# One state's product moved to GpSimd, one product with dt moved by six units, and feed-forward blocks issued together at both ends

## The chip, the core and the metric

The kernel runs on one core of one Trainium2 chip. The engines are called by the names of the profile: PE is TensorE (matmul), DVE is VectorE, ACT is ScalarE, POOL is GpSimd, SP is SyncE, which here only issues DMAs. The metric is the device time of one execution in microseconds (us), lower is better; "time" without more is the median of several executions.

## What is computed

Two layers of a metaformer on x of shape (2, 96, 128, 128). Each layer normalizes over the channels, mixes, adds the result to x, normalizes again, and adds a quantized feed-forward network. Layer 0 mixes with four state-space scans (rows and columns, forwards and backwards), layer 1 with a 3x3 convolution:

```
x = x + mamba4(_ln_c(x))          # four directions, joined by fuse_w
t = t + _L0_ffn_ref(_ln_t(t))     # 96 -> 384 -> 96, fp8 inputs, fp16 accumulator rounding
x = x + conv3x3(_ln_c(x))         # the same 3x3 kernel form as a full 96x96 convolution
t = t + _L1_ffn_ref(_ln_t(t))
```

One scan direction has 192 channels with 16 states each and runs over 16384 positions:

```
h = dA * h + dt_t[:, :, None] * B_t[:, None, :] * u_t[:, :, None]    # dA = exp(dt_t * A)
y = jnp.einsum('bds,bs->bd', h, C_t)
```

then y + D*u, times silu(z), times an output matrix.

## The kernel before

**Order.** For each of the two images, `tile_metaformer` runs `normalize`, then `mamba`, then `ffn_and_conv`. In all three the order of the instructions of each engine is the order in which the program issues them (`in_order`). An engine works strictly through its own list, so a waiting instruction holds back all that stand behind it.

**The scan part, `mamba`.** Two directions run at the same time as a pair (PAIRS): 384 channels in three groups g of 128 partitions. The positions are cut into tiles of T = 512. One **step** is one tile of one pair; there are 64 steps for an image, 128 in all. A step has 24 **units**: 3 groups times 8 pairs of states (g, s), so unit 0 is (0, 0), unit 8 is (1, 0), unit 10 is (1, 4), unit 16 is (2, 0). For unit k the program issues, over several turns of the loop at L486:

- POOL, once for two units (`feed` calls `b_part`, L349): B times dt*u for four states, [128, 4, 512] (L350), and the entry state into the first column (L354, with L353 where s = 0). It is issued two units ahead.
- ACT (`decay`, L360): two exponentials da = exp(dt*A) of [128, 512] into PSUM, issued two units ahead; three such buffers go round (`ps_w`), so the exponentials of unit k+3 write over da of unit k.
- DVE (`scan`, L364): one recurrence for each of the two states.
- `behind` (L453), one unit later: the product with C (L459, DVE, both states in one instruction of 1024 columns), an ACT copy of the last column of h into `hst` (L460), and PE matmuls with the identity that add both states into y (`sums`, L368).

In the six units of BY_POOL (s = 0 and 8 of each group: units 0, 4, 8, 12, 16, 20) the scan writes into the B tile in SBUF instead of PSUM, and POOL makes the product with C (L371, issued at turn k+1); the sums follow at turn k+3. Beside this run the steps of the next tile's preparation, each with a turn: the input matmuls (L218), their copies (L250, L258), two silu passes, each with two table loads (`silu`, L269 to L271; in the steady state they stand at turns 7 and 11), softplus, and `dt_u` (L307): dt times u for one group on POOL, at turns 19, 27 and 29 of the preparation, that is units 19, 3 and 5 of the steps. SP fetches the B and C rows (`row_tile`, L346) into 5 and 4 buffers.

**The part after it, `ffn_and_conv`.** 32 tiles of 512 positions go through four stages: feed-forward of layer 0 (`ffn(0, r)`), layer norm and padding (`to_pad(r)`), convolution (`conv(r)`), feed-forward of layer 1 (`ffn(1, r)`). Each stage is a generator that yields between its short pieces of work. `together` takes a list of (turn at which to begin, generator) and issues one piece of each per turn, in the order of the list; a call of `together` ends when all of its generators have. A feed-forward block has 11 turns: mean removal (xm, L124), square, variance (v, L130), logarithm and exponential, xq (L138), first matrix (L579) in two turns, ReLU, second matrix (L598), copy (L601), and the addition to x on POOL (L604). `to_pad` has the first five of these, the last with three POOL operations (L640 to L643). `conv` issues 12 matmuls (each is two PE instructions), one a turn, and four DVE additions (L625 to L629). The stages are joined by 36 calls, the first and the last four of which hold less than all stages:

```
stages = ((0, 0, partial(ffn, 0)), (4, 4, partial(ffn, 1)), (1, 8, to_pad), (3, 1, conv))
for r in range(NT + 4):
    together(*((at, f(r - lag)) for lag, at, f in stages if 0 <= r - lag < NT))
```

Of the kernel before, what the change touches and what calls it, by code (L numbers as in the profile page):

```python
# [15 lines left out]
ALU = mybir.AluOpType  # L16
# [7 lines left out]
T = 512  # L24
NT = L // T
# [9 lines left out]
ROW_BUFS = (5, 4)  # L35
AHEAD = 2
BY_POOL = tuple((g, s) for g in range(3) for s in (0, 8))
BCO = 32
SEG = 8
NBC = 4 * S  # L40
# [3 lines left out]
def tile_metaformer(ctx: ExitStack, tc: tile.TileContext, a: dict, out: bass.AP):  # L44
    nc = tc.nc
# [94 lines left out]
    def together(*streams):  # L140

        turn = 0
        streams, done = list(streams), object()
        while streams:
            left = []
            for at, g in streams:
                if turn < at or next(g, done) is not done:
                    left.append((at, g))
            streams = left
            turn += 1  # L150
# [40 lines left out]
    def mamba(acc, xnr, xnc, pools, heads):  # L191

        with ExitStack() as st:
            pool = lambda n, bufs, **kw: st.enter_context(tc.tile_pool(name=n, bufs=bufs, **kw))
# [6 lines left out]
            hst = one.tile([128, NG, S], F32, name="hst")  # L201
# [19 lines left out]
            def prologue(pi, i, d):  # L221
# [4 lines left out]
                lo = L - (i + 1) * T if rev else i * T  # L226
# [91 lines left out]
                at = [(-3, 1, load), (3, 0, partial(mix, "xc")), (11, 0, partial(silu, "xc"))]  # L318
# [9 lines left out]
                    at += [(k, 1, partial(softplus, x0, x1))]  # L328
                for g, k in enumerate((14, 24, 25) if first else (14, 15, 16)):
                    at += [(k, 0, partial(dt_in, g)), (k + 1, 0, partial(dt_out, g))]  # L330
                for g, k in enumerate((19, 27, 29)):
                    at += [(k, 0, partial(dt_u, g))]
                    if i > 0:
                        at += [((20, 24, 29)[g], 1, partial(entry, g))]

                outs = (conv_out, gate_out, rows_out, dt_out)
                at = [(k, where, getattr(f, "func", f) not in outs, f) for k, where, f in at]
# [23 lines left out]
                return da  # L361

            def scan(j, da, b, h):
                nc.vector.tensor_tensor_scan(h[:, j, :], da[:, j, :], b[:, j, :], 0.0, ALU.mult, ALU.add)  # L364

            def sums(s, y, c):
                for j in range(2):
                    nc.tensor.matmul(y, ident, c[:, j, :], start=False, stop=s + j == S - 1)  # L368

            def by_pool(h, c):  # L370
                nc.gpsimd.tensor_tensor(c, h, c, ALU.mult)  # L371

            def gated(pi, d, g, y):
                t = d["sz"][:, g, :]
# [26 lines left out]
            def later(k, where, rank, f, *args):  # L401
                todo.setdefault((k, where), []).append((rank, partial(f, *args)))
# [40 lines left out]

            ys = {}

            def gate_before(k):
                pn, pu = divmod(k - 1, nu)
                gated(steps[pn][0], state[pn], units[pu][0], ys.pop(k - 1))
# [4 lines left out]
            def behind(k):  # L453

                n, u = divmod(k, nu)
                (pi, i), d, (g, s) = steps[n], state[n], units[u]
                h, c = hs.pop(k), cs.pop(k)
                if (g, s) not in BY_POOL:
                    nc.vector.tensor_tensor(c, h, c, ALU.mult)  # L459
                nc.scalar.copy(hst[:, g, s : s + 2], h[:, :, T - 1])  # L460
                if s == 0:
                    if k > 0:
                        gate_before(k)
                    y = ps_y.tile([128, T], F32, name="y")
                    nc.tensor.matmul(y, dmat[:, pi, g, :], d["xc"][:, g, :], start=True, stop=False)  # L465
                else:
                    y = ys.pop(k - 1)
                ys[k] = y
                if (g, s) in BY_POOL:
                    later(k + 1, 1, True, by_pool, h, c)  # L470
                    later(k + 3, 1, True, sums, s, y, c)
                else:
                    sums(s, y, c)
                if k == total - 1:
                    gated(pi, d, g, y)
                if s == S - 2 and g > 0:
                    later(k + 4, 0, True, project, pi, i, d, g)
                    later(k + 5, 1, False, collect, pi, d, g)
# [7 lines left out]
            for k in range(total + 6):  # L486
                n, u = divmod(k, nu)
                if u == nu - 3:

                    prepare(n + 2)  # L490
                if k % 2 == 0:
                    fetch(k + 2 * B_AHEAD, 0, bs)
                    feed(k + AHEAD)
                issue(k, 0)
                if k < total:
                    (g, s) = units[u]
                    da, b = das.pop(k), bs.pop(k)
                    hs[k] = b if (g, s) in BY_POOL else da
                    scan(0, da, b, hs[k])
                if 0 < k <= total and not begins(k - 1):  # L500
                    behind(k - 1)
                feed_decay(k + AHEAD)
                if k < total:
                    scan(1, da, b, hs[k])
                if begins(k - 1):
                    behind(k - 1)
                if k % 2 == 0:
                    fetch(k + 2 * C_AHEAD, 1, cs)
                issue(k, 1)

    def ffn_and_conv(b, acc):

        with ExitStack() as st:
# [53 lines left out]
            def ffn(n, r):  # L567

                w1, w2, b1, b2 = layers[n]
                x = acc[:, r * T : (r + 1) * T]  # L570
                xq = wp.tile([C, T], F8, name="xq")
                yield from layernorm(x, eps_t[0:C, 0:1], xq, wp, psp, saturate=False)
                yield
                ph, h16 = [None] * 3, [None] * 3
                hq = wp.tile([128, 3, T], F8, name="hq")

                def up(m):
                    ph[m] = psp.tile([128, T], F32, name="ph", bufs=2)
                    nc.tensor.matmul(ph[m], w1[:, m * 128 : (m + 1) * 128], xq, start=True, stop=True)  # L579

                def half(m):
                    h16[m] = wp.tile([128, T], F16, name="h16", bufs=6)
                    nc.scalar.copy(h16[m], ph[m])

                def relu(m):
                    nc.vector.tensor_scalar(h16[m], h16[m], b1[:, m : m + 1], 0.0, ALU.add, ALU.max)
                    nc.vector.tensor_copy(hq[:, m, :], h16[m], saturate=False)

                up(0), up(1)
                yield  # L590
                half(0), half(1), up(2)
                yield
                relu(0), relu(1), half(2)
                yield
                relu(2)
                po = psp.tile([C, T], F32, name="po", tag="v")
                for m in range(3):
                    nc.tensor.matmul(po, w2[:, m, :], hq[:, m, :], start=m == 0, stop=m == 2)  # L598
                yield
                y16 = wp.tile([C, T], F16, name="y16")  # L600
                nc.scalar.copy(y16, po)  # L601
                yield
                nc.vector.tensor_scalar(y16, y16, b2[:, 0:1], None, ALU.add)  # L603
                nc.gpsimd.tensor_tensor(x, x, y16, ALU.add)  # L604
                if n == 1:
                    nc.sync.dma_start(out[b, :, r * T : (r + 1) * T], x)
                    if b + 1 < NB and r > 4 and r % 4 == 1:
                        read(b + 1, acc, r // 4 - 1)

            def conv(r):  # L610

                seg, lo = segs[r // SEG], r % SEG * R
                x = acc[:, r * T : (r + 1) * T].rearrange("c (n k) -> c k n", k=2)

                def products(name, k0):
                    pc = psp.tile([C, 2, R * half_w], F32, name=name, bufs=1)
                    for k in range(2):
                        for ky in range(3):
                            rows = seg[:, k0 + k, lo + ky : lo + ky + R, :]
                            nc.tensor.matmul(pc[:, k, :], uw[:, k0 + k, ky, :], rows, start=ky == 0, stop=ky == 2)  # L620
                            yield
                    return pc

                outer = yield from products("pc0", 0)
                nc.vector.tensor_tensor(x, x, outer, ALU.add)  # L625
                inner = yield from products("pc1", 2)
                nc.vector.tensor_tensor(x, x, inner[:, 0:1, :].broadcast_to((C, 2, R * half_w)), ALU.add)
                for k, op in enumerate((ALU.add, ALU.subtract)):
                    nc.vector.tensor_tensor(x[:, k, :], x[:, k, :], inner[:, 1, :], op)  # L629
# [17 lines left out]
                    nc.gpsimd.tensor_copy(segs[q - 1][:, :, seg_r + 1, :], segs[q][:, :, 1, :])  # L647

            stages = ((0, 0, partial(ffn, 0)), (4, 4, partial(ffn, 1)), (1, 8, to_pad), (3, 1, conv))
            for r in range(NT + 4):  # L650
                together(*((at, f(r - lag)) for lag, at, f in stages if 0 <= r - lag < NT))

    for b in range(NB):
        xnr = dpool.tile([C, L], F32, name="xnr")
# [78 lines left out]
```

## Time and profile before

| What | us |
|---|---|
| three timed runs | 11155.13, 11156.58, 11157.98; median 11156.58 |
| the profiled execution, its own time | 11158.01 |
| its span, first to last instruction | 11156.2 |
| scan part of each image, 97.8 to 5067.0 and 5660.0 to 10638.0 | 4969.2 and 4978.0 |
| `ffn_and_conv` of each image, 5067.0 to 5582.9 and 10638.0 to 11156.2 | 515.9 and 518.2 |
| one step of the scan part in the steady state | 77.36 |
| busy in the span: PE, DVE, ACT, POOL | 92%, 94%, 71%, 88% |

The page gives busy time per engine over the span; groups of instructions by line with their mean duration; and a chain of work that ended last, followed back from the end, which names at each point the engine that the end really depended on. The trace behind it answers the same for a stretch of time: a list of one engine's instructions with start, duration and the idle time ahead of them, or the pieces of the chain within the stretch. An instruction's duration is longer than the distance to the next one where the engine overlaps them: the 512 column scans last 1.22 us and start every 1.12 us.

### The profile page before, as it was taken

How to read it: one execution, taken by the hardware profiler on the slowest of the kernel's cores; microseconds unless marked ns; L12 is line 12 of the kernel's file. 1: busy time of each engine (PE TensorE's matmuls, PEld its weight loads, DVE VectorE, ACT ScalarE, POOL GpSimd, SP SyncE). 2: the span in 40 equal slices, each digit the busy share in tenths (PEclk: the TensorE clock that was granted, in tenths of full speed). 3: DMA queues.
4: the chain of work that ended last, by engine and by line, in shares of the span. 5: the costliest groups of instructions: out<-in, count | busy, mean ns of one | idle time of the engine just before them, and what ended most of it. 6: DMA issues, size and time to landing. Idle time of an engine off the chain costs nothing.

```text
span 11156.2 us, 94135 instructions
## 1 busy us (share of the span) xinstructions
PE 10260.0 (92%) x24592; PEld 3999.1 (36%) x24592; DVE 10498.1 (94%) x10337; ACT 7927.3 (71%) x13564; POOL 9803.2 (88%) x4908
## 2 busy tenths in 40 slices
PE   8999999999999999998989999999999999999988
PEld 3333333333333333334433333333333333333344
DVE  7999999999999999996579999999999999999955
ACT  6777777777777777775677777777777777777756
POOL 6999999999999999993269999999999999999932
PEclk9999999999999999999999999999999999999999
DMA  8888888888888888881178888888888888888800
GB/s 307 340 336 338 344 338 342 335 339 344 336 344 336 339 343 336 341 337 45 29 283 340 340 339 342 337 337 343 339 340 339 336 344 339 340 339 336 341 31 15
DMA packets 540497, 3416.18 MB, mean 306 GB/s; under 512 B 67469, under 2 KB 68589, under 8 KB 143577
## 3 DMA queue, kind: packets, MB, share of 16 engines
q1 hardware_dynamic: 539160, 3408.84, 78.0%
q8 instruction: 199, 3.26, 0.1%
q14 instruction: 338, 2.76, 0.1%
q10 hardware_dynamic: 800, 1.31, 0.0%
HBM read 3288.26 MB, written 54.53 MB: 300 GB/s over the span
## 4 chain that ended last, share of the span: by engine, by line
DVE 55%; issue 18%; ACT 18%; PE 8%; DMA 0%; POOL 0%; DVEq 0%; SPq 0%; POOLq 0%; ACTq 0%
DVE da L364 33%; DVE row L364 10%; DVE row L459 9%; ACT da L360 5%; ACT L270 3%; ACT L271 3%; PE pc L620 2%; PE v L130 2%; PE xm L124 2%; ACT xc L270 2%; ACT sz L270 2%; PE ph L579 1%; DVE sz L375 1%; ACT xc L250 1%; ACT mix L258 1%
## 5 line engine op out<-in xcount | busy, mean ns | idle before, releaser
L350 POOL TENSOR_TENSOR row<-dtu,row 128x2048 f32<-128x2048 f32 x1536 | 6950.6, 4526 | 7.5 <-DMA row<-bcd 7.0
L368 PE MATMUL y<-row,ident 128*128 128x512 f32 x12288 | 5684.5, 602 | 360.8 <-DVE row L459 350.8
L364 DVE TENSOR_TENSOR_SCAN da<-da,row 128x512 f32<-128x512 f32 x4608 | 5497.9, 1216 | 82.4 <-ACT da L360 35.0
L360 ACT ACTIVATE da<-dt,amat 128x512 f32<-128x512 f32 x6144 | 4247.9, 693 | 176.6 <-DVE row L364 6.3
L368 PEld LDWEIGHTS y<-row,ident 128*128 128x128 f32 x12288 | 2251.2, 190 | 3668.3 <-issue 2249.7
L459 DVE TENSOR_TENSOR row<-da,row 128x1024 f32<-128x1024 f32 x2304 | 2772.2, 1203 | 0.0
L371 POOL TENSOR_TENSOR row<-row,row 128x1024 f32<-128x1024 f32 x768 | 1806.5, 2352 | 271.0 <-issue 149.0
L460 ACT COPY hst<-da 128x2 f32<-128x2 f32 x2304 | 373.5, 162 | 2272.4 <-DVE row L459 2269.5
L364 DVE TENSOR_TENSOR_SCAN row<-da,row 128x512 f32<-128x512 f32 x1536 | 1849.6, 1204 | 34.4 <-DMA row<-bcd 32.1
L218 PE MATMUL misc<-xa,inx 96*64 96x512 f32 (+1 forms) x2048 | 935.1, 599 | 13.2 <-ACT dt L300 6.4
L218 PE MATMUL misc<-xb,inx 96*64 96x512 f32 (+1 forms) x2048 | 935.0, 599 | 1.6 <-ACT xc L250 1.6
L309 POOL TENSOR_TENSOR dtu<-dt,xc 128x512 f32<-128x512 f32 x384 | 488.2, 1271 | 188.1 <-ACT dt L304 102.3
L604 POOL TENSOR_TENSOR acc<-acc,y 96x512 f32<-96x512 f32 x128 | 147.1, 1149 | 547.0 <-DVE y L603 547.0
L383 PE MATMUL misc<-acc,ident 96*96 96x512 f32 x512 | 388.2, 843 | 222.1 <-ACT hst L460 199.3
L218 PEld LDWEIGHTS misc<-xa,inx 96*64 96x64 f32 (+1 forms) x2048 | 323.9, 163 | 581.1 <-issue 474.1
L465 PE MATMUL y<-xc,dmat 128*128 128x512 f32 x768 | 420.1, 628 | 110.5 <-DVE sz L375 110.5
L295 PE MATMUL misc<-rows,dtw 12*128 12x512 f32 x768 | 434.0, 645 | 64.4 <-ACT dt L300 35.5
L385 PE MATMUL misc<-sz,gmat 128*96 128x512 f32 x1024 | 483.6, 594 | 0.0
L620 PE MATMUL pc<-seg,uw 96*96 96x256 f32 x1536 | 424.5, 381 | 1.9 <-POOL seg L640 1.9
L218 PEld LDWEIGHTS misc<-xb,inx 96*64 96x64 f32 (+1 forms) x2048 | 323.4, 163 | 251.1 <-issue 186.3
L354 POOL TENSOR_TENSOR row<-row,enter 128x4 f32<-128x4 f32 x1488 | 298.2, 200 | 116.5
L277 PE MATMUL misc<-xc,bcw 128*96 128x512 f32 x768 | 355.8, 600 | 7.2 <-ACT xc L270 7.2
(92 smaller groups left out, 7423.0 us busy)
## 6 DMA issues: line engine op xcount, KB each, us to landing
row<-bcd SPq DMA_DIRECT2D x3072, 1024.0 KB, 7.4
xc<-mix SPq DMA_DIRECT2D x252, 128.0 KB, 4.8
sz<-mix SPq DMA_DIRECT2D x252, 128.0 KB, 4.8
xa<-xnr SPq DMA_DIRECT2D x124, 193.1 KB, 5.1
xb<-xnc SPq DMA_DIRECT2D x124, 193.1 KB, 5.5
bcd<-rows SPq DMA_DIRECT2D x126, 128.0 KB, 4.2
acc<-in_x_dram SPq DMA_DIRECT2D x16, 768.0 KB, 5.7
xnr<-xn SPq DMA_DIRECT2D x16, 768.0 KB, 4.9
```

The costliest lines, as they stand in the source:

```text
L218: nc.tensor.matmul(ps[rows, :], w(PAIRS[pi][d], k, lo, hi), src[d][:, k : k + T], **se)
L270: nc.scalar.activation(d[name], d[name], AF.Silu)
L295: nc.tensor.matmul(d["ps"], w, d["rows"][0 : 2 * RK, :], start=True, stop=True)
L309: nc.gpsimd.tensor_tensor(dtu, d["dt"][:, g, :], d["xc"][:, g, :], ALU.mult)
L350: nc.gpsimd.tensor_tensor(b, d["dtu"][g][:, None, :].broadcast_to((128, 4, T)), b, ALU.mult)
L360: nc.scalar.activation(da[:, j, :], d["dt"][:, g, :], AF.Exp, scale=amat[:, pi, g, s + j : s + j + 1])
L364: nc.vector.tensor_tensor_scan(h[:, j, :], da[:, j, :], b[:, j, :], 0.0, ALU.mult, ALU.add)
L368: nc.tensor.matmul(y, ident, c[:, j, :], start=False, stop=s + j == S - 1)
L371: nc.gpsimd.tensor_tensor(c, h, c, ALU.mult)
L385: nc.tensor.matmul(d["po"], gmat[:, pi, 2 * g - 2 + k, :], d["yg"][g - 1 + k], start=False, stop=k == 1)
L459: nc.vector.tensor_tensor(c, h, c, ALU.mult)
L620: nc.tensor.matmul(pc[:, k, :], uw[:, k0 + k, ky, :], rows, start=ky == 0, stop=ky == 2)
```

## The change

1. `HALF_POOL` names one unit, (1, 4), which is unit 10. Its first state is scanned into the B tile and multiplied by C on POOL (512 columns, issued at turn k+1 = 11); its second state stays as it was, with a DVE product of 512 columns instead of 1024. The one ACT copy into `hst` becomes two copies of one column each. The first state's sum on PE moves to turn k+3 = 13.
2. `dt_u` of group 2 moves from turn 29 to turn 35 of the preparation: from unit 5 to unit 11 of the step, ahead of the new POOL product.
3. In `ffn_and_conv` the first three calls of `together` become one and the last four become one. In the last one `conv` issues three matmuls per turn instead of one.

```
+HALF_POOL = ((1, 4),)
...
-                for g, k in enumerate((19, 27, 29)):
+                for g, k in enumerate((19, 27, 35)):
                     at += [(k, 0, partial(dt_u, g))]
...
-            def sums(s, y, c):
-                for j in range(2):
+            def sums(s, y, c, states=(0, 1)):
+                for j in states:
                     nc.tensor.matmul(y, ident, c[:, j, :], start=False, stop=s + j == S - 1)
 
-            def by_pool(h, c):
-                nc.gpsimd.tensor_tensor(c, h, c, ALU.mult)
+            def product(engine, h, c, states):
+                if len(states) == 2:
+                    engine.tensor_tensor(c, h, c, ALU.mult)
+                for j in states if len(states) == 1 else ():
+                    engine.tensor_tensor(c[:, j, :], h[:, j, :], c[:, j, :], ALU.mult)
...
+            def by_pool(g, s):
+                return (0, 1) if (g, s) in BY_POOL else (0,) if (g, s) in HALF_POOL else ()
...
-                h, c = hs.pop(k), cs.pop(k)
-                if (g, s) not in BY_POOL:
-                    nc.vector.tensor_tensor(c, h, c, ALU.mult)
-                nc.scalar.copy(hst[:, g, s : s + 2], h[:, :, T - 1])
+                (da, b), c = hs.pop(k), cs.pop(k)
+                pool = by_pool(g, s)
+                rest = tuple(j for j in (0, 1) if j not in pool)
+                if rest:
+                    product(nc.vector, da, c, rest)
+                for h, states in ((b, pool), (da, rest)):
+                    if states:
+                        lo, hi = states[0], states[-1] + 1
+                        nc.scalar.copy(hst[:, g, s + lo : s + hi], h[:, lo:hi, T - 1])
...
-                if (g, s) in BY_POOL:
-                    later(k + 1, 1, True, by_pool, h, c)
-                    later(k + 3, 1, True, sums, s, y, c)
-                else:
-                    sums(s, y, c)
+                if pool:
+                    later(k + 1, 1, True, product, nc.gpsimd, b, c, pool)
+                    later(k + 3, 1, True, sums, s, y, c, pool)
+                if rest:
+                    sums(s, y, c, rest)
...
-            def conv(r):
+            def conv(r, burst=1):
...
-                            yield
+                            if (3 * k + ky + 1) % burst == 0:
+                                yield
...
-            for r in range(NT + 4):
-                together(*((at, f(r - lag)) for lag, at, f in stages if 0 <= r - lag < NT))
+            together(*((2 * r, ffn(0, r)) for r in range(3)), (11, to_pad(0)), (13, to_pad(1)))
+            for r in range(3, NT):
+                together(*((at, f(r - lag)) for lag, at, f in stages if 0 <= r - lag))
+            together(
+                (0, to_pad(NT - 1)), *((at, ffn(1, NT - 4 + k)) for k, at in enumerate((0, 5, 11, 15))),
+                *((at, conv(NT - 3 + k, 3)) for k, at in enumerate((0, 6, 10))),
+            )
```

More of the change, by code (lines that the diff above doesn't have):

```diff
@@ L363, in scan @@
             def scan(j, da, b, h):
-                nc.vector.tensor_tensor_scan(h[:, j, :], da[:, j, :], b[:, j, :], 0.0, ALU.mult, ALU.add)
-            def sums(s, y, c):
-                for j in range(2):
+                nc.vector.tensor_tensor_scan(h[j], da[:, j, :], b[:, j, :], 0.0, ALU.mult, ALU.add)
+            def sums(s, y, c, states=(0, 1)):
+                for j in states:
                     nc.tensor.matmul(y, ident, c[:, j, :], start=False, stop=s + j == S - 1)
-            def by_pool(h, c):
-                nc.gpsimd.tensor_tensor(c, h, c, ALU.mult)
+            def product(engine, h, c, states):
[3 more added lines that the diff above has]
+                    engine.tensor_tensor(c[:, j, :], h[:, j, :], c[:, j, :], ALU.mult)
             def gated(pi, d, g, y):
@@ L497, in mamba @@
                     da, b = das.pop(k), bs.pop(k)
-                    hs[k] = b if (g, s) in BY_POOL else da
-                    scan(0, da, b, hs[k])
+                    hs[k] = da, b
+                    h = [(b if j in by_pool(g, s) else da)[:, j, :] for j in range(2)]
+                    scan(0, da, b, h)
                 if 0 < k <= total and not begins(k - 1):
@@ L503, in mamba @@
                 if k < total:
-                    scan(1, da, b, hs[k])
+                    scan(1, da, b, h)
                 if begins(k - 1):
```

## The prediction

> **What bounds the kernel now.** I read the shares of the chain first. DVE is 94% busy, but the chain gives it 55% and ACT 18%, though ACT is only 71% busy. So somewhere the end waits for ACT.
>
> ```profile
> DVE 55%; issue 18%; ACT 18%; PE 8%; DMA 0%; POOL 0%; DVEq 0%; SPq 0%; POOLq 0%; ACTq 0%
> ```
>
> POOL has 0%: in the steady state nothing waits for its 88%. Then I took the chain's pieces in one step of the scan part, and looked for where ACT enters. In this step unit 10's first scan starts at 2075.00, unit 13's at 2085.37.
>
> ```profile
> 2075.00 0.06 DVE da L364
> 2075.06 1.08 issue
> 2076.14 1.22 DVE row L459
> 2077.36 0.02 issue
> 2077.38 0.17 ACT hst L460
> 2077.55 0.02 issue
> 2077.57 0.70 ACT da L360
> 2078.28 0.02 issue
> 2078.30 0.69 ACT da L360
> 2079.00 0.61 ACT xc L250
> 2079.60 0.02 issue
> 2079.62 1.28 ACT L270
> 2080.90 0.01 issue
> 2080.91 1.49 ACT xc L270
> 2082.41 0.02 issue
> 2082.42 1.28 ACT L271
> 2083.70 0.01 issue
> 2083.72 0.17 ACT hst L460
> ```
>
> The reader should see what is missing. The chain leaves DVE with the product of unit 9 (2076.14) and stays on ACT: copy, exponentials of unit 12, xc, silu between two table loads, unit 10's hst copy, and (2083.91 to 85.34) the exponentials of unit 13. It comes back to DVE at 2085.37. DVE's product of unit 10, at 2079.51, is not on it. DVE's own list shows the wait at its return (last bracket):
>
> ```profile
> 2079.51 1.21 DVE L459 TENSOR_TENSOR row<-da,row 128x1024 f32<-128x1024 f32 x1
> ...
> 2085.37 1.23 DVE L364 TENSOR_TENSOR_SCAN da<-da,row 128x512 f32<-128x512 f32 x1 [0.17 <-ACT da L360]
> ```
>
> The other ACT stretch runs from unit 6's product (2065.97) to 2075.00, through the other silu; DVE waits 0.24 there. Some steps name POOL's L371 as releaser of that wait; but at 4086.26 the same scan starts before that POOL product ends (4084.08 + 2.35 = 4086.43), so it is ACT. Both waits recur every 77.36 us in the five stretches I read, so one step is DVE from 2085.37 to the next unit 6, then ACT, a little DVE, and ACT.
>
> For the feed-forward ends I read the engines' lists and the granted clock by stretch.
>
> ```profile
> 5069.50:5113.90 44.40, 32.68 (x47) 9.52 (x48) 11.05 (x27) 17.65 (x30) 8.07 (x10) 0.50 0.00 0
> 5113.90:5570.00 456.10, 423.44 (x1479) 218.03 (x1477) 277.39 (x637) 303.26 (x507) 136.46 (x156) 1.00 0.09 26
> ```
>
> After span and length come the busy times of PE, PEld, DVE, ACT, POOL, then the clock: 0.50 in the first calls, 1.00 afterwards. The first three calls are one dependent chain after another at half PE clock.
>
> **1. The product of unit 10.** DVE's 1024 columns take 1.12 from start to start; the nearest row for 512 columns with a PSUM input is L375, 0.59. So DVE does 0.53 less a step. It reaches unit 13's first scan at about 84.6 instead of 85.1, and waits there for ACT until 85.37 as before: worth 0. The cover is ACT's stretch; without it the edit is worth 126 x 0.53 = 67 (126 steps, 63 an image, hold the next step's silu).
>
> The second hst copy stands on that stretch, ahead of unit 13's exponentials. A copy from SBUF in a packed ACT stream moves the next instruction by 0.08 (L460 at 2086.82, next at 2086.90), one from PSUM ahead of exponentials by 0.19 (2083.72 to 83.91). The new copy is from SBUF, so I take 0.08: **+10** (126 x 0.08 = 10.1). Bounds: 0 (it vanishes in the pipeline after the table load) and 126 x 0.19 = 24. Queued behind its wait are those exponentials; it waits for a scan that ended before 2076.3, so not at all.
>
> POOL's 512 columns cost about 1.2 (L371's 2.35 halved, L309's 1.27). A step of POOL from 2007.98 to 2085.33 is 77.35, of which I count 2.30 idle ahead of its L371s: 75.05 + 1.2 = 76.25 of work, below 77.4. By turns, with dt*u moved away: unit 4's product starts at 59.3 (was 60.55), unit 8's B rows end at 66.6 (was 67.8; needed 68.2), unit 8's product runs from 71.8 to 74.1, unit 12's rows until 78.85, dt*u until 80.1, the new product until 81.3, unit 14's rows until 86.1 (needed 87.8), unit 12's product until 88.4 (0.7 later than now), unit 16's rows until 93.3 (needed 94.6). Then 0.77 and 0.50 of idle time at units 16 and 0 absorb the rest. The product's input, unit 10's first scan, ends at 76.2. What is queued behind it, unit 14's rows, keeps 1.7 us. So 0.
>
> Buffers: the C tile of units 10 and 11 waits for a sum at turn 13 (about 87 instead of 84.5), and SP's fetch for unit 18, issued at turn 14, behind it. Landing takes 7.4 (median of the DMA list), so about 95; DVE needs it at 105. The B tile is free at 84 and refilled at turn 14. PE does the same two passes later; its 71.76 of 77.36 leave room. 0 each.
>
> **2. dt x u to unit 11.** It passes the products of units 4 and 8 and the rows of units 8 to 12 on POOL, no DMA. Its first reader, unit 16's rows, begins at 88.4, it ends at 80.1. Alone it is worth 0: nothing waited for POOL. It is the room for the new product.
>
> **3. First calls.** Now PE's first xm starts at 5067.77 and `to_pad(1)` reaches POOL (L640) at 5110.15. Joined, the chain is: block 0 as now up to xq (5073.5); xm, v of blocks 1 and 2 fill PE in between; block 2 ends behind blocks 0 and 1 because ACT does for each 0.59 + 1.32 + 1.64 + 0.58 = 4.1 and DVE 3.3, strictly by turns; then two paddings. Walking the 18 turns with PE's half-clock rows (xm 1.72, v 1.8, L579 0.43 a matmul, L598 1.3 for three from start to start), block 0's addition ends at 5086.6, block 2's at 5092.5, and L640 of `to_pad(1)` starts at 5097.2: 13 earlier. With the full-clock rows (0.86, 0.9, 0.22, 0.65) it is 5094.2: 16 earlier; the next call starts warm and gains about 1 more. I take 15 and, as the second image's third and fourth calls were already 0.9 quicker (40.25 against 41.17 from its first to its fourth L604), 14. Bounds 12 (half clock, no gain after) and 20 (no queueing between blocks).
>
> The Trainium skill ("TensorE: Matmul & The Clock Gate", Part 1, What's actually happening) says that PE's clock doubles after a free-running window of about 3.4 us of sustained activity. The rows agree in direction: PE went to full clock only after about 8 us without a gap (5105.95 to 5114), and stayed at half with 0.7 gaps. By the page alone the joined call would warm in its middle, and its saving would be near 16.
>
> **4. Last calls.** Now the last conv matmuls of the 32nd call are followed by four calls; the last addition ends at 5582.89, 11.0, 10.4, 10.75 and 10.96 apart. Joined: `to_pad(31)` begins at 5536.0, its POOL part at 5544.5; convolution 29 ends at 47.2, 30 at 56.75, 31 at 64.9. Each convolution needs about 5.2 of PE (12 x 0.43) plus 1.46 of DVE, and PE interleaves it with the blocks, so they follow one another about 8 to 10 apart; this, not the 26 turns, sets the pace. The last block's xm starts at 65.0. From xm to the end the last block now takes 12.46 (5570.43 to 5582.89, clock 0.56), plus about 0.7 for block 30 beside it: 78.2, 4.7 earlier; I take 4.5 an image. Bounds 0 (dense matmuls delay the paddings' squares by as much) and 7 (full clock). The output DMAs and the next image's reads move with the additions; normalization starts when PSUM is free, so it moves too.
>
> The skill's "SBUF — State Buffer" (Who interferes with whom) says that DVE copies and scalar operations in two-port modes and POOL block one another wholly. L603 took 0.35 with POOL idle and 0.55 beside L643. By the page, three blocks with POOL additions (1.15) could lose up to 3 us in the joined first call; that would leave about 12.
>
> **Sum**, against the profiled execution's own 11158.0 (span 11156.2 and 1.8 around it): - 15 - 14 - 2 x 4.5 + 10 = -28, so 11130; 1.4 less for the median of the runs (11156.6): **11129**.
>
> **Rivals.**
> - *DVE is the bound after all*, as its 94% says. Then 67 come on top and no copy counts: -38 - 67 = -105, 11052. Against it: the wait of unit 13 exists already, with the full product in place. Chance 0.07.
> - *POOL's new product comes late* (slower). If it waits until all four scans of its B tile are done (81.84 instead of 76.2), it ends near 83.1, unit 14's rows at 87.85, unit 12's product at 90.2, unit 16's rows at 95.1 against 94.6: DVE waits 0.5 more each step, with the copy 0.6: 126 x 0.6 = +75, less 38: 11194. It decides once the product starts after about 81.5. Against it: unit 12's product starts 0.13 after its own second scan (85.20 to 85.33), while unit 13's scans, on the same tile, still run. Chance 0.07.
> - *The ends give little, or the joined calls don't overlap*, the change not doing what it says: two xm buffers in PSUM hold the third block until the first has its xq, and the dense convolutions delay the padding. With 8 an image instead of 19: -16 + 10, 11151. Chance 0.06.
> - My forecast's case: 0.80. Its bounds: ends -24 to -54, copies 0 to +24: -54 to 0, so 11103 to 11157.
>
> **How the numbers follow.** About 22 us (0.2%) is what a measurement of this kernel can tell from no change. Within my case -28 lies just beyond it; of its width I give 0.7 to beyond -22 and the rest to within: 0.56 faster, 0.24 same. With the first rival: faster 0.63; the third adds to same: 0.30; slower 0.07. The range 11097 to 11162 holds my case with a margin of 5 for the walks of the ends, and the third rival; it leaves out the first and second, 0.14.
>
> **What would show it.** Unit 13's first scan waiting about 0.7 to 0.9 for ACT's exponentials in each step, a step of 77.4 to 77.5, POOL busy 1.2 more a step: step 1 right. A step of 76.8: wrong, DVE was the bound. A scan that waits for L350: the second rival. From the first xm to L640 of the second padding 26 to 30 instead of 42.4, and from the 32nd call's end to the last addition about 42 instead of 47: steps 3 and 4 right.

## The result, and the profile after

The changed kernel takes 11263.8 us (median of five runs, 11253.5 to 11267.6) against 11156.6 before: ratio 1.0094, 95% interval 1.008 to 1.0108. It is slower, outside the range that I gave and on the side to which I gave 0.07. The profiled execution has a span of 11251.7, 95.5 more than before. (In what follows the changed kernel's lines stand 1 to 14 below the numbers of the kernel before: scan L365, exponentials L361, DVE product L373 for 1024 columns and L375 for 512, sums L369, gate L379, dt's matmul L296, hst L472, feed-forward addition L617, padding L654.)

Where the 95.5 come from, by the first xm of each feed-forward part and its last addition:

| Part | before | after | change |
|---|---|---|---|
| start to the first xm, image 0 | 5067.8 | 5137.5 | +69.7 |
| first xm to the end of the last addition, image 0 | 515.1 | 492.7 | -22.4 |
| from there to the next first xm (normalization and scan), image 1 | 5056.8 | 5125.9 | +69.1 |
| first xm to the end of the last addition, image 1 | 513.5 | 492.6 | -20.9 |

So the joined calls brought 43, about what was forecast (38), and the scan part, forecast at +10, lost 139. DVE's list in two steps of the changed kernel says at once which of my readings held and what is new (last bracket: idle time and who ended it):

```profile
2111.67 3.61 DVE L365 TENSOR_TENSOR_SCAN da<-da,row 128x512 f32<-128x512 f32 x3 [0.76 <-ACT da L361]
2127.77 0.69 DVE L379 TENSOR_TENSOR sz<-y,sz 128x512 f32<-128x512 f32 x1 [1.13 <-PE y L369]
```

The first line is unit 13's scan. It now waits 0.76 for ACT instead of 0.17: the shorter product only lengthened DVE's wait, as forecast. The second line is new: the gate after unit 15, which multiplies the finished y by silu(z), waits for PE's last sum. Over the span (engine, line, releaser; total, times, longest):

```profile
DVE sz L379 <- PE y L369: 126.0, 79, 2.8
...
DVE da L365 <- ACT da L361: 100.5, 128, 2.5
```

Before, the gate (L375 there) hardly waited for PE:

```profile
DVE sz L375 <- PE y L368: 0.8, 2, 0.6
```

The waits now occur in some steps only, as 1.13 to 1.18 or 2.78 to 2.79. Steps without one show the change's own price: from 4064.48 to 4141.90 at unit 10 is 77.42, against 77.36.

Why PE is late is in its own list. First the kernel before, from unit 12 on:

```profile
2086.88 1.88 PE L368 MATMUL y<-row,ident 128*128 128x512 f32 x4
2088.87 1.12 PE L295 MATMUL misc<-rows,dtw 12*128 12x512 f32 x2
2090.15 1.99 PE L368 MATMUL y<-row,ident 128*128 128x512 f32 x4 [0.15 <-DVE row L459]
2092.40 1.12 PE L295 MATMUL misc<-rows,dtw 12*128 12x512 f32 x2 [0.27 <-ACT dt L300]
2093.51 3.70 PE L368 MATMUL y<-row,ident 128*128 128x512 f32 x8
```

The same stretch of the changed kernel:

```profile
2111.74 2.74 PE L369 MATMUL y<-row,ident 128*128 128x512 f32 x6
2115.02 1.12 PE L296 MATMUL misc<-rows,dtw 12*128 12x512 f32 x2 [0.55 <-ACT rows L284]
2116.45 3.34 PE L369 MATMUL y<-row,ident 128*128 128x512 f32 x4 [0.31 <-DVE row L373]
2119.73 1.41 PE L296 MATMUL misc<-rows,dtw 12*128 12x512 f32 x2
2121.07 3.70 PE L369 MATMUL y<-row,ident 128*128 128x512 f32 x8
```

Four instructions that took 1.99 take 3.34, right after PE has idled 0.55 and 0.31 with a matmul between that contracts over only 12 rows (`12*128` in its line). The granted clock, the last value but two of a stretch's row, falls with them (2.5 to 2 us long stretches of the changed kernel; busy PE, PEld, DVE, ACT, POOL, then the clock):

```profile
2112.00:2114.50 2.50, 2.47 (x6) 0.76 (x4) 2.46 (x3) 2.44 (x6) 2.42 (x3) 1.00 1.01 419
2118.00:2120.00 2.00, 2.00 (x4) 0.50 (x3) 2.00 (x3) 0.81 (x4) 1.92 (x4) 0.50 0.98 365
```

In the steady steps of the changed kernel (here and below: steps 2 to 63 of each image, 124 in all) the record of granted clock holds 77 stretches at half speed, 3.41 or 6.83 long, 341 us in all; in the kernel before it holds none. Their two lengths go with the two waits: the short stretch here is followed by the 1.13, and one of 6.83 from about 4158 (5.21 for the eight instructions that took 3.70) by a wait of 2.78 at 4170.07. This holds without exception: 54 of the 124 steps have a stretch of 3.41 and a gate wait of 1.13 to 1.18, 23 have one of 6.83 and a wait of 2.78 or 2.79, and 47 have neither.

Which steps are hit goes by where a stretch can begin. All 77 begin at whole multiples of 3.413 from one another. Where such a point falls 1.55 to 2.64 after the start of the first dt matmul, just after both gaps, a half-clock stretch begins; in the 47 steps without one it falls 0.63 to 1.55 after it.

### The profile page after: what moved, and what is told of

Read it like the earlier page. It is cut to its first block, busy times and chain, and to the rows that moved or that the text cites. A ratio compares the mean times of both kernels' runs of the same rounds, so it can differ in the third digit from the quotient of the medians.

```text
span 11251.7 us, 94775 instructions
## 1 busy us (share of the span) xinstructions
PE 10388.0 (92%) x24592; PEld 4038.5 (36%) x24592; DVE 10443.8 (93%) x10337; ACT 7905.0 (70%) x13692; POOL 9962.6 (89%) x5036
## 5 line engine op out<-in xcount | busy, mean ns | idle before, releaser
L351 POOL TENSOR_TENSOR row<-dtu,row 128x2048 f32<-128x2048 f32 x1536 | 6950.8, 4526 | 7.7 <-DMA row<-bcd 7.4
L369 PE MATMUL y<-row,ident 128*128 128x512 f32 x12288 | 5819.3, 614 | 317.1 <-DVE row L373 280.0
L365 DVE TENSOR_TENSOR_SCAN da<-da,row 128x512 f32<-128x512 f32 x4480 | 5342.7, 1216 | 128.0 <-ACT da L361 100.5
L361 ACT ACTIVATE da<-dt,amat 128x512 f32<-128x512 f32 x6144 | 4232.1, 691 | 172.3 <-DVE row L365 6.4
L369 PEld LDWEIGHTS y<-row,ident 128*128 128x128 f32 x12288 | 2283.0, 192 | 3683.8 <-issue 2308.3
L373 DVE TENSOR_TENSOR row<-da,row 128x1024 f32<-128x1024 f32 x2176 | 2619.4, 1204 | 0.0
L365 DVE TENSOR_TENSOR_SCAN row<-da,row 128x512 f32<-128x512 f32 x1664 | 2008.8, 1207 | 61.4 <-DMA row<-bcd 31.6
L373 POOL TENSOR_TENSOR row<-row,row 128x1024 f32<-128x1024 f32 x768 | 1805.8, 2351 | 228.7 <-issue 212.5
L472 ACT COPY hst<-da 128x2 f32<-128x2 f32 (+1 forms) x2304 | 368.7, 160 | 2316.0 <-DVE row L373 2312.3
L617 POOL TENSOR_TENSOR acc<-acc,y 96x512 f32<-96x512 f32 x128 | 147.4, 1152 | 522.2 <-DVE y L616 463.9
L296 PE MATMUL misc<-rows,dtw 12*128 12x512 f32 x768 | 462.0, 682 | 99.2 <-ACT rows L284 71.3
L379 DVE TENSOR_TENSOR sz<-y,sz 128x512 f32<-128x512 f32 x384 | 262.5, 684 | 128.2 <-PE y L369 126.0
```

The costliest lines, as they stand in the source:

```text
L296: nc.tensor.matmul(d["ps"], w, d["rows"][0 : 2 * RK, :], start=True, stop=True)
L351: nc.gpsimd.tensor_tensor(b, d["dtu"][g][:, None, :].broadcast_to((128, 4, T)), b, ALU.mult)
L361: nc.scalar.activation(da[:, j, :], d["dt"][:, g, :], AF.Exp, scale=amat[:, pi, g, s + j : s + j + 1])
L365: nc.vector.tensor_tensor_scan(h[j], da[:, j, :], b[:, j, :], 0.0, ALU.mult, ALU.add)
L373: engine.tensor_tensor(c, h, c, ALU.mult)
```

## The experiments

The theory after the result: the half product lets PE finish the sums around unit 10 earlier, so that its idle time, which stood ahead of unit 10's sums (0.79 at 2080.76; now 0.25), moves to the narrow dt matmul, and PE's clock falls there. The rivals: dt x u's later turn; PE having too much queued before the gate; the joined calls.

**Each half alone.** `ends_only` is the kernel before with the new loop of `ffn_and_conv`; `scan_only` has only the scan part's edits; `dtu_only` and `half_only` split those:

```
dtu_only:   enumerate((19, 27, 29)) -> enumerate((19, 27, 35)), nothing else
half_only:  scan_only with enumerate((19, 27, 29))
```

> Before, with only the joined first and last calls of the feed-forward part. In the profile of the changed kernel that part is 22.4 us shorter in each image (515.1 to 492.7 from the first xm to the last addition), so if the two halves of the change don't act on one another: 11156.6 - 45 = 11112. If the joined calls are to blame for the loss (through what they leave behind for the next part), it comes out above 11156.

> Before, with only the edits of the scan part (half product on GpSimd, dt x u at unit 11). If the whole loss is in the scan part: 11264 + 45 = about 11309, with DVE waiting for PE at L379 (the gate, 126 us in the changed kernel). If the loss needs both halves: about 11165 (only the copy's 8).

> Before, with only dt x u of the last group at unit 11. My theory (PE's clock falls because the half product leaves PE's idle time bunched after unit 12) gives 11157 and no half-clock stretch in the steady steps. Rival, the later dt x u delays GpSimd's product of unit 12 and with it the sums that the gate waits for: 11250 to 11310.

> Before, with only the half product of unit 10 on GpSimd, dt x u left at unit 5. My theory: half-clock stretches as in the changed kernel, 11280 to 11310. Rival (the later dt x u is the cause): about 11165. A third possibility: GpSimd, now late from unit 5 on, makes DVE wait for the B rows of unit 8 or 16 (L351) instead.

| Run | us (median) | ratio to before, 95% interval | half-clock time in the steady steps |
|---|---|---|---|
| ends_only | 11119.7 | 0.9967, 0.9954 to 0.998 | 0 |
| scan_only | 11300.7 | 1.0131, 1.0114 to 1.0148 | 352 |
| dtu_only | 11153.5 | 0.9998, 0.9989 to 1.0007 | 0 |
| half_only | 11303.0 | 1.0132, 1.0117 to 1.0148 | 348 |

`ends_only` came out 8 above the 11112 expected; its five times spread from 11112 to 11128. The two halves of the change add up (-36 and +144 to +107), and the later dt x u is worth nothing either way. The half product alone does the harm, with the same waits at the gate (133 us in its profile). The rivals of dt x u and of the joined calls fall.

**Does the clock cause it, or the amount of work?** Two ways to keep the clock without touching the half product. `dup_rows` gives PE 0.9 us more work in each step, so that it has less time to idle:

```
+                    nc.tensor.matmul(d["ps"][0 : BCO + NBC, :], bcw[:, pi, 0, :], d["xc"][:, 0, :], start=True, stop=True)
                     for g in range(NG):
```

> The changed kernel with one matmul more in each step: the first of the three matmuls of L278 is issued twice (the first result is overwritten), which gives PE 0.9 us more work just ahead of its 0.55 gap before dt's matmul (L296). Clock theory: the gap closes, the clock stays at 1.00 through the steady steps, the gate's waits (126 us) go, and the kernel gets faster by work added: 11115 to 11150. Rival, PE simply has too much queued ahead of the gate: each step gets 0.9 us more wait, 11264 + 113 = about 11375.

It takes 11123.7, ratio 0.9971 (0.996 to 0.9982); no half-clock stretch in the steady steps, and the gate's waits for PE shrink to 0.3 in all. PE's list shows the gap of 0.55 ahead of dt's matmul closed (no bracket):

```profile
2087.13 2.74 PE L370 MATMUL y<-row,ident 128*128 128x512 f32 x6
2089.80 1.12 PE L297 MATMUL misc<-rows,dtw 12*128 12x512 f32 x2
2091.00 1.98 PE L370 MATMUL y<-row,ident 128*128 128x512 f32 x4
```

More work on a late engine made the kernel some 140 us faster than the changed one. That a queue was too long is refuted.

`dt_in96` leaves the number and the order of PE's instructions as they are and changes only how many rows dt's matmul reads (with one memset at the start for the zero weights):

```
-                    nc.tensor.matmul(d["ps"], w, d["rows"][0 : 2 * RK, :], start=True, stop=True)
+                    nc.tensor.matmul(d["ps"], w, d["rows"], start=True, stop=True)     # dtw: 96 rows, the others zero
```

> The changed kernel with dt's matmul (L296) contracting over all 96 rows of its input instead of 12; the added weight rows are zero. Same duration expected (1.12 a pair). If what drops the clock counts how much of the array is busy, and not only whether a matmul runs, these three matmuls in the gap's neighbourhood keep it at 1.00 and the time falls to 11115 to 11150. If only idle time counts, nothing changes: 11264 within 15.

It takes 11123.6 (0.9971, 0.9959 to 0.9982), again with no half-clock stretch. PE's list in that run:

```profile
2089.34 1.12 PE L298 MATMUL misc<-rows,dtw 96*128 96x512 f32 x2 [0.56 <-ACT rows L286]
2090.78 1.98 PE L371 MATMUL y<-row,ident 128*128 128x512 f32 x4 [0.31 <-DVE row L375]
2093.02 1.13 PE L298 MATMUL misc<-rows,dtw 96*128 96x512 f32 x2 [0.26 <-ACT dt L303]
```

The gaps of 0.56 and 0.31 are those of the changed kernel, and the pair still takes 1.12; but the four sums after it take 1.98 instead of 3.34. So it is not idle time alone that drops the clock here: a matmul on 12 rows next to it counts less than one on 96. The control, and a size between:

> Control: the kernel before, with dt's matmul over 96 rows. Its clock already stood at 1.00 through the steady steps, so by the clock theory nothing changes: 11157 within 8. If the wider matmul is faster in itself, it shows here too: 11125 or less, and then the dt_in96 run proves nothing on the clock.

> The changed kernel with dt's matmul (L296) contracting over 32 rows, 20 of them with zero weights, between the 12 of the changed kernel (about 11264) and the 96 at which the clock held (11124). If the rows that a matmul uses weigh in proportion: a window of 3.41 us with 0.56, 0.31 and 1.12 of L296 has 42% idle or nearly idle at 12 rows, and the threshold lies somewhere above the 25% of idle time that 96 rows leave; 32 rows may land on either side, and half-clock stretches in only some steps (11150 to 11250) are likeliest. If 12 rows are under a fixed granule that 32 fills: 11124.

`before_dt96` takes 11155.3 (0.9999, 0.999 to 1.0009): the wider matmul gains nothing where the clock already stood, so what it gained above was the clock. `dt_in32` takes 11124.8 (0.9972, 0.9962 to 0.9982) with no half-clock stretch: my "likeliest" for it, a loss in some steps, was wrong. 32 rows are already enough. (A sum in that expectation is off: 0.56, 0.31 and 1.12 are 58% of 3.41; 42% is what is left.) Nor is it luck with the points at which a stretch can begin: in `dt_in96` and in `dt_in32` these points (carried on from the few stretches outside the steady steps) fall at all distances from 0 to 3.4 after the first dt matmul in the 124 steps, and no step lost its clock. So the gaps alone (`dt_in32`, `dt_in96`) and the 12-row matmul alone (before, `dup_rows`) leave the clock at 1.00; the two together drop it. Whether rows weigh in proportion with a threshold between, or in groups of which 12 rows fill less than one, these runs don't tell.

**Is the place of the half product what made it worthless?** By the prediction's reading, DVE's 0.53 should count anywhere in the stretch that DVE sets. `u14`, `u2` and `u18_dt96` move it there; `u2_dt96` and `u18_dt96` also have the 96 rows:

```
HALF_POOL = ((1, 12),)    # u14; its sum at turn k + 2, ahead of unit 15's
HALF_POOL = ((0, 4),)     # u2
HALF_POOL = ((2, 4),)     # u18
```

> The changed kernel with the half product at unit 14 instead of unit 10 (its sum on PE at turn 16, ahead of unit 15's). Unit 14's product lies in the stretch that DVE sets (2085.37 to 2142.1 in the profile before), so by the chain its 0.53 counts: 126 x 0.53 = 67, less 13 for a copy if it counts: 11112 - 54 to - 67 = 11045 to 11058, if the clock holds. If the clock falls as it did at unit 10: 11180 or more. If GpSimd can't keep up (76.25 of work in a step of 76.83): waits for L351 and about 11100.

> The changed kernel with the half product at unit 2. Also in DVE's stretch: 11045 to 11058 if clock and GpSimd hold. GpSimd is tighter here than at unit 14 (dt x u of group 1 stands at unit 3, next to the new product; unit 8's rows would end within 0.1 of their need), so 11050 to 11110 with waits for L351 is likelier. If moving any sum to a later turn drops the clock: 11180 or more.

> The half product at unit 2 and dt's matmul over 96 rows together, on the changed kernel. The clock held in all but three stretches at unit 2 alone (11078), so little is left to gain: 11070 to 11080. If the 0.30 that its gate still waits for PE comes from those narrow matmuls, up to 126 x 0.3 = 38 less.

> The half product at unit 18, clock kept by the 96 row matmul, on the changed kernel. Also in DVE's stretch: up to 67 below 11124 by the chain, so 11057 to 11080. GpSimd has dt x u of group 0 and the new product side by side at unit 19, and by its walk unit 0's rows end 0.1 after their need: 11070 to 11100 with waits for L351 if so.

| Run | us | ratio to before, 95% interval |
|---|---|---|
| u14 | 11103.1 | 0.9952, 0.9936 to 0.9969 |
| u2 | 11077.9 | 0.9929, 0.9914 to 0.9944 |
| u2_dt96 | 11072.4 | 0.9927, 0.9911 to 0.9944 |
| u18_dt96 | 11066.4 | 0.992, 0.9905 to 0.9934 |

All three places beat `ends_only`, by 17 to 53 us, where unit 10 with the clock kept (11123.6) is 4 slower than `ends_only`. The step is 77.00 in u2 and 76.98 in u18_dt96 against 77.33 in ends_only, so 0.33 to 0.35 of the 0.53 arrive. None of the four has a half-clock stretch in its steady steps (the three that the expectation of u2_dt96 counts at unit 2 lie in the last steps of the images). Where the rest went can be read from the times at which scans start, beside the same places in ends_only.

- *u14*: the expectation was missed by 45. The half product saves its 0.53, but the gate after unit 15 waits 0.34 for PE in each step (43 us in all), and the scan behind it starts 0.45 later than without that wait; 0.08 is left.
- *u2*: unit 10's first scan no longer waits for ACT (0.23 in ends_only). The gate after unit 7, which stands just ahead of it, waits instead:

```profile
2065.46 0.69 DVE L379 TENSOR_TENSOR sz<-y,sz 128x512 f32<-128x512 f32 x1 [0.30 <-PE y L369]
```

  In this step unit 10's first scan comes 13.71 after unit 6's, in ends_only 13.50: 0.21 are lost, which is what is missing. The gate's waits are 39 us in all; the wider matmul left them at 39.5, so they don't come from dt's matmuls.
- *u18_dt96*: the gates wait 0.3 in all, but unit 0's first scan waits for GpSimd in each step:

```profile
1953.65 1.22 DVE L367 TENSOR_TENSOR_SCAN da<-da,row 128x512 f32<-128x512 f32 x1
1954.95 1.22 DVE L367 TENSOR_TENSOR_SCAN row<-da,row 128x512 f32<-128x512 f32 x1
1954.71 0.20 POOL L357 TENSOR_TENSOR row<-row,enter 128x4 f32<-128x4 f32 x1
```

  It starts 1.30 after the scan ahead of it instead of 1.12, as the last instruction for its B rows ends (1954.71 + 0.20). The scans around it lose 0.18 in the median step, all that is missing. The lists show no wait under 0.15, so this one has no bracket.

So the waits for GpSimd's rows that I had thought likely are there, if not at L351: at unit 0 in u18_dt96, and as short a one at unit 8 in u2, where the gate waits anyway. This account of u14, u2 and u18_dt96 is read from the traces; no run removed these waits. u18_dt96 is the fastest version measured.

## Why the prediction was wrong, point by point

- **DVE's half product is worth 0 at unit 10: right.** 0.76 of wait instead of 0.17, and the kernel with the clock kept (dt_in96) is no faster than without the scan edits (ends_only). The same edit at units 2 and 18 does gain 0.33 to 0.35 a step, which is the reading of the chain confirmed from the other side. The first rival (DVE is the bound, 11052) fell for this unit.
- **The second hst copy, 0.08 a step: right, 0.10.** ACT's list of the changed kernel:

```profile
2109.94 0.19 ACT L472 COPY hst<-row 128x1 f32<-128x1 f32 x1
2110.04 0.15 ACT L472 COPY hst<-da 128x1 f32<-128x1 f32 x1
2110.23 1.42 ACT L361 ACTIVATE da<-dt,amat 128x512 f32<-128x512 f32 x2
```

  One more copy moves the exponentials of unit 13 by 0.10. The step grows by 0.06, so 126 x 0.06 = 8 instead of 10.
- **GpSimd keeps up: right.** The new product takes 1.26 (forecast 1.2); no scan waits for L351. The second rival, the only case on the slower side, fell: the product follows dt x u at once (5011.02, 5012.25). The price came from a mechanism that I had not listed.
- **The step that failed** is in part 1, under Buffers: "PE does the same two passes later; its 71.76 of 77.36 leave room. 0 each." The room was there; a sum over a step was the wrong test. What counted was where PE's idle time lies within a few us. I had the granted clock in hand, and a rule on it, but used both only at the feed-forward ends, because the clock was 1.00 in all steady steps before. The 0 stands against the gate's waits of 126 us, most of the +139 in the scan part.
- **The Trainium skill's rule.** "TensorE: Matmul & The Clock Gate" (Part 1, What's actually happening) has the clock fall after at least one idle window of about 3.4 us. The lengths agree: half-clock stretches of 3.41 and 6.83. The condition doesn't: in the 3.41 ahead of one such stretch (2113.53 to 2116.94) matmuls are recorded for 2.55. The measurement decides: a window need not be idle.
- **First calls: right in kind, a little too small.** From the first xm to the second padding's L654 it is 25.98 (5137.45 to 5163.43) instead of 42.38: 16.4 saved, 15 forecast. The half-clock walk was the wrong end: most of the joined call ran warm, as the variance's 1.10 instead of 2.02 shows.

```profile
5142.29 1.10 PE L131 MATMUL v<-sq,mean_w 96*96 96x512 f32 x2 [1.06 <-ACT sq L128]
```

- **Last calls: right.** From the last addition of the 32nd call to the start of the last one 38.56 (5590.43 to 5628.99) instead of 43.19: 4.6 saved, 4.5 forecast. The fourth call, now begun at full clock, gained another 1.4 in the first image (8.57 instead of 9.97 from the second padding to the fourth addition). So the ends brought 22.4 and 20.9 instead of 19.5 and 18.5. The Trainium skill's "SBUF — State Buffer" (Who interferes with whom), by which the prediction feared up to 3 us in the first call, cost nothing that shows here: the three L616 of that call (L603 before) took 0.34 or 0.35, as with POOL idle.

## What to carry to other kernels

Before crediting an edit on the busiest engine, find the piece of the chain that it stands on: the same half product was worth nothing at unit 10 and some 50 us at unit 18. Then look at what the edit does to the idle time of an engine that waits for it: PE's total was unchanged (71.80 and 71.85 a step), but its gaps moved next to a narrow matmul, the clock fell for 3.41 or 6.83 us in 77 of 124 steps, and the late sum came back as a wait of DVE. Where the granted clock drops in a stretch that looks busy, try wider contractions of the same length (zero rows) or a little more work, before reordering anything.

## What the runs showed of the hardware that was not expected

- A PE that is recorded busy for 2.55 of 3.41 us was put to half clock when 1.12 of that was a matmul contracting over 12 rows; with 32 or 96 rows in the same place, the same gaps and the same duration, it stayed at full clock in every steady step (0 against 341 us of half clock). Longer single gaps elsewhere in the step (1.56 and 1.38 ahead of matmuls over 96 and 128 rows, 4096.30 and 4108.59) never dropped it.
- Adding 0.9 us of PE work per step removed all but 0.3 of 126 us of waiting and made the kernel faster than the change without it (11123.7 against 11263.8).
- Half-clock stretches are multiples of 3.41 long and begin on one grid of 3.413 through the whole run. The same gaps gave none, one or two of its intervals by where the grid fell, and a wait of 0, about 1.13 or about 2.78. The average steady step of the changed kernel is 78.51, 23 intervals of the grid (78.51), where the step without a wait is 77.42: so the waits seem to hold the step to the grid, which no run tests.
